# Products with adj in a stack of graph layers: Strassen's four-pass float32 matmuls replaced by three single-pass products of split operands

## The chip, the cores and the metric

The kernel runs on one core of one Trainium2 chip. The metric is the device time of one launch in microseconds (us), lower is better. The profile is one execution taken by the hardware profiler; its span runs from the first to the last instruction.

## What is computed

32 samples of 512 nodes with 128 features go through four layers that share one 512x512 matrix adj. Each layer normalizes x, applies a ReLU, runs a graph network and adds the result to x. Cut to what matters here:

```python
# layer 0: normalized adjacency, then a 128x128 weight
h = relu(layernorm(x));  A = d[:, None] * (adj + eye) * d[None, :]
x = x + einsum('nm,bmc->bnc', A, h) @ W.T + b
# layer 1: five gated steps
h = relu(layernorm(x))
for _ in range(5):
    m = einsum('nm,bmd->bnd', adj, h);  av = concat([m, m])
    z = sigmoid(av @ w3.T + u3(h));  r = sigmoid(av @ w4.T + u3(h))
    hv = tanh(av @ w5.T + (r * h) @ u5.T)
    h = (1 - z) * h + z * hv
x = x + h
# layers 2 and 3: graph attention with masks adj + eye != 0 and adj > 0
```

So a sample needs six products of a 512x512 matrix with a 512x128 one: one with the normalized matrix, five with adj. All inputs and outputs are float32.

## The kernel before, in words

Everything lies in SBUF as tiles of 128 partitions x 512 float32 elements, one tile for one sample. A sample's product with the 512x512 matrix is done for two samples at once, in `products` (line 604). It is Strassen's scheme on 2x2 blocks: VectorE makes four combinations of the two samples' halves (L616), TensorE makes seven block products, each of two matmuls of 128x256 float32 elements (L628), ScalarE copies four partial sums out of PSUM (L633), and VectorE adds three results together (L641). The combinations of the constant matrix are made once by `right_factors` (line 399), for adj and for the normalized matrix. The first four samples of layer 0 use a plain float32 product instead (`product`, L668).

`ggnn` (line 732) runs the five steps of a pair of samples, and `step` (line 755) one step of one sample: gate matmuls (L759, L760), a tanh on ScalarE (L762), r times h on VectorE (L764), matmuls for z (L766) and for the candidate (L773, L774), two more tanh (L768, L776) and three VectorE operations for the new h (L778 to L781). The new h is feature-major and has to be turned for the next product. VectorE turns 32x32 blocks (L570), and DMAs move them through DRAM and back (`shuttle`, line 564). In the first and last steps TensorE turns it instead (`to_features`, L560). `gat` (line 828) does an attention layer; its masked exponentials are L891 and its mixing matmuls L917.

Nothing loops on the chip. The program calls `op(engine, cost, due, emit, reads, writes)` for each piece of work, and `Plan` (line 47) writes out a fixed order for each engine: among the operations whose inputs are there and whose tiles are free, the one with the earliest due slot goes first. Each name in the dictionary at line 274 is a pool of tiles, so its number of tiles limits how far the work of one sample can run ahead. `LANES` (6) limits the samples under way in layer 1. A due of `STEPS * b` puts sample b five slots after the one before it, and each step of a sample six slots (`LANES`) after the last. From `IDLE_FROM` on the planner fills waits of TensorE with transposes of nothing. The order is fixed at build time; on the chip an engine waits on semaphores for the others, and what lies behind a waiting instruction waits too.

The numbers in `op` are the planner's, not measurements. The order in which work for a pair is written is:

```python
for s in range(STEPS):
    now = due + LANES * s
    ms = products(*hs, of_adj, now)
    for i, b in enumerate(pair):
        hs[i], hTs[i] = step(b, s, ms[i], hTs[i], now + i, lanes[i])
```

Of the kernel before, what the change touches and what calls it, by code (L numbers as in the profile page):

```python
# [11 lines left out]
BF16 = mybir.dt.bfloat16  # L12
# [3 lines left out]
P = 128  # L16
# [8 lines left out]
IDLE_FROM = 1420  # L25
RUN_UP = 8
LANES = 6


class Val:  # L30


    def __init__(self, kind, parts=1):
        self.kind, self.uses, self.t = kind, 0, None
        self.writers, self.readers = [[] for _ in range(parts)], [[] for _ in range(parts)]
# [11 lines left out]
class Plan:  # L47
# [42 lines left out]
    SLOT = 10.3  # L90
# [63 lines left out]
    def attempt(self):  # L154
# [80 lines left out]
        while events:  # L235
            now, _, kind, o = heapq.heappop(events)
            if kind == 2:
                pass
            elif kind == 0:
                busy[o.engine] = False  # L240
                settle(o, True)
            else:
                done += o.id is not None
                settle(o, False)
                for v in o.vals:
                    v.uses -= 1
                    if not v.uses and v.kind:
                        free[v.kind].append(v.t)
            for e in ready:
                start(e)  # L250
# [5 lines left out]
def gnn_stack(ctx: ExitStack, tc: tile.TileContext, a: dict, out: bass.AP):  # L256
# [13 lines left out]
    def flat(t):  # L270
# [6 lines left out]
        "x": tiles(13, TOKENS, "x"),  # L277
        "h": tiles(LANES, [P, 2, 2 * D], "h"),
# [4 lines left out]
        "pair": tiles(3, [P, 2, 2 * D], "pair"),  # L283
        "m": tiles(LANES + 1, TOKENS, "m"),
        "S": tiles(2, [P, 4, 2 * D], "S"),
        "half": tiles(6, [P, 2 * P], "half"),
# [9 lines left out]
        "e": tiles(3, [P, C, N], "e"),  # L296
        "v": tiles(2, TOKENS, "v"),
        "mask": tiles(2, [P, N], "mask", dtype=BF16),
# [6 lines left out]
    }, [(167, 0.1), (181, 0.05)], 1300,  # L305
        IDLE_FROM, lambda v: nc.tensor.transpose(v.t[:, 0, :], ident.t, ident.t))
    op = plan.op
    MM, MM1, TURN = 0.858, 0.224, 0.111
# [13 lines left out]
    def load(name, shape, src, due, queue="SP", cost=0.45, delay=4.7):  # L322
        v = fixed(shape, name)
        q = {"SP": nc.sync, "POOL": nc.gpsimd, "AQ": nc.scalar}[queue]
        op(queue if queue != "AQ" else "ACT", cost, due, lambda: q.dma_start(v.t, src), w=[v], delay=delay)
        return v

# [26 lines left out]
    w0 = load("w0", [P, D], a["L0_gnn_W"], -993.9, delay=5.6)  # L354
# [4 lines left out]
    for k in ("w4", "w3", "w5", "u3", "u5"):  # L359
        src = a[f"L1_gnn_{k}_w"]  # L360
        raw[k] = load(k, [P, src.shape[1]], src, -994.5 if k in ("w4", "w3") else -993.3)
# [12 lines left out]
    adjT = fixed([P, C, N], "adjT", C)  # L374
    deg, dinv = fixed(SMALL, "deg", C), fixed(SMALL, "dinv")
# [23 lines left out]
    def right_factors(mT, due, passing=False):  # L399

        made = Val("e", 4) if passing else fixed([P, C, N], "made", 4)

        def quarter(a, n):
            return mT.t[:, 2 * a:2 * a + 2, n * 2 * P:(n + 1) * 2 * P]
        f = {0: (lambda: quarter(0, 0), mT), 3: (lambda: quarter(1, 0), mT), 5: (lambda: quarter(1, 1), mT)}
        f |= {k: (lambda i=i: made.t[:, i].rearrange("p (k n) -> p k n", k=2), made[i]) for i, k in enumerate((2, 1, 4, 6))}
        for k, u, v in ((2, (0, 1), 0), (1, (1, 1), 2), (4, (1, 1), None), (6, (1, 0), 1)):
            op("DVE", 0.62, due, lambda k=k, u=u, v=v: nc.vector.tensor_sub(  # L410
                f[k][0](), quarter(*u), quarter(0, 1) if v is None else f[v][0]()),
               r=[mT, *([f[v][1]] if v else [])], w=[f[k][1]])
        return f
    of_adj = right_factors(adjT, -3.6)
# [14 lines left out]
    def transposed(dues, *group, then=()):  # L429
# [5 lines left out]
        for i, (parts, _) in enumerate(group):  # L435
            def turns(i=i, parts=parts):
                for k, (v, at, sign) in enumerate(parts):
                    nc.tensor.matmul(p.t[:, i, :], v.t[:, at:at + D], sign.t, start=k == 0, stop=k == len(parts) - 1)
# [109 lines left out]
    def chunk(h, c):  # L548

        if h.kind not in ("h", "pair"):  # L550
            return h.t[:, c, :]
        return h.t.rearrange("p a (f l) -> p a l f", l=2)[:, c // 2, c % 2, :]
# [11 lines left out]
    def shuttle(src, squares, dst, halves, due, soon):  # L564
# [3 lines left out]
        if halves:  # L568
            for a in range(2):
                op("DVE", 0.34, soon, lambda a=a: nc.vector.transpose(  # L570
                    sq.t.rearrange("p q (a j l) -> p a q l j", a=2, l=2)[:, a],
                    flat(src.t).rearrange("p (a l q i) -> p a q l i", a=2, l=2, q=Q)[:, a]), r=[src], w=[sq])
        else:
            op("DVE", 0.61, soon, lambda: nc.vector.transpose(
                sq.t.rearrange("p q (c j) -> p q c j", c=C), flat(src.t).rearrange(squares, c=C, q=Q)), r=[src], w=[sq])
# [3 lines left out]
        if halves:  # L579
            for a in range(2):  # L580
                op("SP", 0.4, due, lambda a=a: nc.sync.dma_start(
                    dst.t[:, a, :].rearrange("p (k f) -> p k f", k=Q),
                    far.t.rearrange("q i k (a f) -> a (q i) k f", a=2)[a]), r=[far], w=[dst[a]], delay=5)
        else:
            op("SP", 0.4, due, lambda: nc.sync.dma_start(
                dst.t if dst.kind != "h" else dst.t.rearrange("p a (k f) -> p (a k) f", k=2), far.t.rearrange("q i k f -> (q i) k f")),
               r=[far], w=[dst], delay=5)

    def shuttle_first(h, hT, due, soon):

        sq, far = Val("sq"), Val("far", Q)
        for a in range(2):
            op("DVE", 0.34, soon, lambda a=a: nc.vector.transpose(
                sq.t.rearrange("p k (a l i) -> p a k l i", a=2, l=2)[:, a],
                h.t.rearrange("p a (k j l) -> p a k l j", k=Q, l=2)[:, a]), r=[h[a]], w=[sq])
# [8 lines left out]
    def products(h1, h2, factors, due):  # L604

        x1, x2, S = (h1[0], h1[1]), (h2[0], h2[1]), Val("S", 4)
        HV, HM, HA = 0.34, 2 * 0.432, 0.26

        def part(item):
            v, a = item
            return v.t[:, a, :]

        def combine(o, u, v, f):
            op("DVE", HV, due - 5, lambda: f(part(o), part(u), part(v)), r=[u, v], w=[o])  # L616
        add, sub = nc.vector.tensor_add, nc.vector.tensor_sub
        combine(S[2], x1[0], x2[0], sub)
        combine(S[0], x2[0], x2[1], add)
        combine(S[1], S[0], x1[0], sub)  # L620
        combine(S[3], x1[1], S[1], sub)
        m1, m2, p1, u2, u4, r, t = Val("m", 2), Val("m", 2), Val("half"), Val("half"), Val("half"), Val("bank"), Val("bank")

        def times(r, item, k, fresh, *also):
            def two():
                u = part(item).rearrange("p (f l) -> p l f", l=2)
                for l in range(2):
                    nc.tensor.matmul(low(r), u[:, l, :], factors[k][0]()[:, l, :], start=fresh and l == 0, stop=l == 1,  # L628
                                     skip_group_check=not fresh)
            op("PE", HM, due, two, r=[item, factors[k][1]], w=[r, *also])  # L630

        def copy(o, r, out):
            op("ACT", HA, due - 6, lambda: nc.scalar.copy(out(), low(r)), r=[r], w=[o])  # L633

        def low(v):
            return flat(v.t)[:, :2 * P]

        def high(v):
            return flat(v.t)[:, 2 * P:]
        def add_up(o, u, out):  # L640
            op("DVE", HV, due - 5, lambda: nc.vector.tensor_add(out(), u.t, low(t)), r=[u, t], w=[o])  # L641

        times(r, x1[0], 0, True, m1, m2, t, p1, u2, u4)
        copy(p1, r, lambda: p1.t)
        times(t, x1[1], 3, True)
        add_up(m1[0], p1, lambda: low(m1))
        times(r, S[1], 1, False)
        copy(u2, r, lambda: u2.t)
        times(t, S[2], 4, True)
        times(r, S[0], 2, False)  # L650
        copy(u4, r, lambda: u4.t)
        add_up(m2[1], u4, lambda: high(m2))
        times(t, x2[1], 6, False)
        add_up(m2[0], u2, lambda: low(m2))
        times(r, S[3], 5, False)
        copy(m1[1], r, lambda: high(m1))
        return m1, m2

# [15 lines left out]
    def normalized(begun):  # L674

        anT = fixed([P, C, N], "anT", C)
        drow = Val("bank")
# [15 lines left out]
        return anT, right_factors(anT, -16.5, True)  # L693
# [4 lines left out]
    def gcn(pair, due):  # L698
        first, ys = pair[0] < 4, []
        for i, b in enumerate(pair):  # L700
            y = Val("y", C) if first else Val("pair", 2)
# [8 lines left out]
        ms = [product(y, due + i) for i, y in enumerate(ys)] if first else products(*ys, factors["an"], due + 1)  # L710
        if b == 1:
            factors["anT"], factors["an"] = normalized(ms[0])
# [19 lines left out]
    def ggnn(pair, due):  # L732
        hs, hTs, lanes = [], [], []
        for b in pair:
            lane, h, hT = Val("lane"), Val("h", 2), Val("hT", Q)
# [280 lines left out]
```

The softmax here doesn't subtract the row's maximum and nothing guards it: scores larger than these inputs give would overflow.

## Time and profile before

| | |
|---|---|
| median of 3 runs | 1618.6 us (1618.34 to 1618.92) |
| span of the profiled execution | 1616.2 us |
| TensorE clock granted | 1.000 of full speed |
| VectorE records, start to end | 1379.3 us busy |
| ScalarE records, start to end | 723.0 us busy |
| share of the 16 DMA engines by queue q1 | 39.9% |
| instructions | 24006 |

The profiled execution's span is 2.4 us shorter than the median of the runs; times out of the profile are compared with 1616.2, and the forecast adds the difference. A row of a group reads: line, engine, operation, names written and read, shapes, count, then the busy time in us and the mean in ns of one, then the idle time just before these instructions and what ended it. The ends of matmul records are modelled, so their starts carry more than their lengths. A float32 matmul appears as two records. In the windows a line gives a stretch, its length, the busy time and the count of each of five engines, the clock, the DMA share and GB/s.

### The profile page before, as it was taken

The numbers are of one execution on the slowest core, as the hardware profiler recorded it, in microseconds if no ns is written. First come the engines' busy times: TensorE is split into PE (matmuls) and PEld (weight loads), VectorE is DVE, ScalarE is ACT, GpSimd is POOL, SyncE is SP. The second block draws the span as 40 slices with busy tenths as digits, with TensorE's granted clock in tenths as the row PEclk, the third lists the DMA queues.
The fourth block names the chain that finished last, engine by engine and source line by source line (L and its number), as shares of the span: only waits on it lengthen the run. The fifth ranks groups of instructions, "written<-read, shape, count | busy, mean of one in ns | idle before, by whom it ended". The sixth has DMA issues, their size and how long they took to land.

```text
span 1616.2 us, 24006 instructions
## 1 busy us (share of the span) xinstructions
PE 1609.5 (100%) x7314; PEld 1166.0 (72%) x7314; DVE 1379.3 (85%) x3981; ACT 723.0 (45%) x1622; POOL 143.1 (9%) x137
## 2 busy tenths in 40 slices
PE   9999999999999999999999999999999999999998
PEld 8676667777767777777777767767767767667778
DVE  8977687888898988888989788998887978888888
ACT  5644444535354354443545345353353444443444
POOL 2210000110000001001001011010000100000000
PEclk9999999999999999999999999999999999999999
DMA  4233453443444444363543535445354353434111
GB/s 131 46 85 83 100 129 87 116 108 96 120 97 117 101 122 100 92 143 82 118 110 87 136 86 119 100 98 127 92 118 98 79 124 83 101 98 118 34 33 41
DMA packets 382850, 159.83 MB, mean 99 GB/s; under 512 B 208288, under 2 KB 364288, under 8 KB 382720
## 3 DMA queue, kind: packets, MB, share of 16 engines
q1 hardware_dynamic: 382432, 157.77, 39.9%
q8 instruction: 58, 0.95, 0.3%
q14 instruction: 72, 0.59, 0.1%
q10 hardware_dynamic: 288, 0.52, 0.1%
HBM read 87.30 MB, written 70.89 MB: 98 GB/s over the span
## 4 chain that ended last, share of the span: by engine, by line
PE 96%; DVE 2%; DMA 1%; ACT 0%; issue 0%; SPq 0%; DVEq 0%; ACTq 0%
PE bank L628 35%; PE bank L917 12%; PE bank L759 8%; PE bank L760 8%; PE bank L774 8%; PE bank L766 8%; PE bank L773 8%; PE bank L849 3%; PE bank L718 2%; PE bank L668 1%; PE bank L903 1%; DVE e L891 1%; PE bank L560 1%; DMA e<-in_adj_dram 0%; DMA maskT<-far_mask 0%
## 5 line engine op out<-in xcount | busy, mean ns | idle before, releaser
L493 POOL TENSOR_TENSOR rstd<-ve,mhalf 128x4 f32<-128x4 f32 x119 | 131.8, 1108 | 1375.9 <-DVE ve L485 1054.9
L628 PE MATMUL bank<-made,S 128*128 128x256 f32 x960 | 231.4, 380 | 0.1
L917 PEld LDWEIGHTS bank<-h_gat,e 128*128 128x128 f32 x1792 | 210.2, 191 | 16.4 <-issue 13.6
L917 PE MATMUL bank<-h_gat,e 128*128 128x129 f32 x1792 | 211.9, 275 | 0.0
L633 ACT COPY half<-bank 128x256 f32<-128x256 f32 x282 | 104.2, 370 | 238.7 <-PE bank L628 237.0
L628 PEld LDWEIGHTS bank<-made,S 128*128 128x128 f32 x960 | 184.1, 196 | 31.4 <-issue 12.0
L762 ACT ACTIVATE r<-bank,gate_bw 128x512 f32<-128x512 f32 x160 | 109.5, 685 | 192.5 <-PE bank L760 168.4
L778 DVE TENSOR_TENSOR hv<-hv,hT 128x512 f32<-128x512 f32 x160 | 109.4, 684 | 76.7 <-ACT hv L776 76.5
L776 ACT ACTIVATE hv<-bank,gate_bw 128x512 f32<-128x512 f32 x160 | 109.5, 684 | 127.3 <-PE bank L774 121.6
L759 PE MATMUL bank<-m,wT 128*128 128x512 f32 x320 | 163.6, 593 | 0.0
L766 PE MATMUL bank<-m,wT 128*128 128x512 f32 x320 | 163.4, 592 | 0.0
L774 PE MATMUL bank<-rh,wT 128*128 128x512 f32 x320 | 163.4, 592 | 0.0
L760 PE MATMUL bank<-hT,wT 128*128 128x512 f32 x320 | 163.4, 592 | 0.0
L773 PE MATMUL bank<-m,wT 128*128 128x512 f32 x320 | 163.4, 592 | 0.0
L891 DVE SCALAR_TENSOR_TENSOR e<-row,h_gat,maskT 128x512 f32<-128x512 f32 x224 | 160.1, 738 | 0.0
L764 DVE SCALAR_TENSOR_TENSOR rh<-r,hT 128x512 f32<-128x512 f32 x160 | 109.6, 685 | 58.4 <-ACT r L762 57.0
L628 PE MATMUL bank<-adjT,h 128*128 128x256 f32 x640 | 158.5, 379 | 0.0
L628 PEld LDWEIGHTS bank<-adjT,h 128*128 128x128 f32 x640 | 123.4, 196 | 26.7 <-issue 15.1
L641 DVE TENSOR_TENSOR m<-half,bank 128x256 f32<-128x256 f32 x282 | 115.8, 411 | 30.6 <-ACT half L633 15.7
L768 ACT ACTIVATE z<-bank,gate_bw 128x512 f32<-128x512 f32 x160 | 109.5, 684 | 59.3 <-PE bank L766 56.7
L480 DVE BATCH_NORM_STATS2 st<-x 128x6 f32<-128x128 f32 x480 | 115.6, 277 | 6.8 <-DMA x<-in_x_dram 6.6
L760 PEld LDWEIGHTS bank<-hT,wT 128*128 128x128 f32 x320 | 60.8, 190 | 76.5 <-issue 76.0
(144 smaller groups left out, 2353.4 us busy)
## 6 DMA issues: line engine op xcount, KB each, us to landing
far<-sq SPq DMA_DIRECT2D x936, 64.0 KB
h<-far SPq DMA_DIRECT2D x244, 128.0 KB
gT<-far SPq DMA_DIRECT2D x56, 256.0 KB
row<-line SPq DMA_DIRECT2D x56, 256.0 KB
x<-in_x_dram SPq DMA_DIRECT2D x32, 256.0 KB
hT<-far SPq DMA_DIRECT2D x112, 64.0 KB
h<-far SPq DMA_DIRECT2D x28, 256.0 KB
out_dram<-x SPq DMA_DIRECT2D x28, 256.0 KB
```

What stands on the lines that cost most here:

```text
L480: op("DVE", 0.21, due, lambda c=c: nc.vector.bn_stats(st.t[:, c, :], xb.t[:, c, :]), r=[xb[c]], w=[st[c]])
L493: op("POOL", 1.0, due, lambda: nc.gpsimd.tensor_tensor(rstd.t, ve.t, mhalf.t, ALU.pow), r=[ve, mhalf], w=[rstd])
L628: nc.tensor.matmul(low(r), u[:, l, :], factors[k][0]()[:, l, :], start=fresh and l == 0, stop=l == 1, skip_group_check=not fresh)
L641: op("DVE", HV, due - 5, lambda: nc.vector.tensor_add(out(), u.t, low(t)), r=[u, t], w=[o])
L759: nc.tensor.matmul(flat(gate.t), gates.t[:, 0, :], flat(m.t), start=True, stop=False)
L760: nc.tensor.matmul(flat(gate.t), gates.t[:, 1, :], flat(hT.t), start=False, stop=True)
L764: op("DVE", V, due - 5, lambda: nc.vector.scalar_tensor_tensor(flat(rh.t), flat(r.t), 1.0, flat(hT.t), op0=ALU.add, op1=ALU.mult), r=[r, h ...
L766: op("PE", MM, due + 0.3, lambda: nc.tensor.matmul(flat(gate.t), gates.t[:, 2, :], flat(m.t), start=False, stop=True, skip_group_check=Tru ...
L773: nc.tensor.matmul(flat(cand.t), gates.t[:, 3, :], flat(m.t), start=True, stop=False)
L774: nc.tensor.matmul(flat(cand.t), u5T.t[:, 0, :], flat(rh.t), start=False, stop=True)
L891: op("DVE", 0.68, due + 3, lambda j=j: nc.vector.scalar_tensor_tensor(e.t[:, j, :], rows(row.t), h.t[:, j, D + 1:D + 2], mask(j), op0=ALU. ...
L917: nc.tensor.matmul(pt()[:, c, :D + 1], e.t[:, j, i * P:(i + 1) * P], h.t[:, j, :D + 1], start=(j == 0), stop=(j == C - 1))
```

## The change

Strassen's scheme goes. Each operand of a product is split exactly into an upper part (its first twelve significant bits, by an integer AND with -4096) and a lower part (the rest). Three products are made of these parts, of a type that TensorE multiplies in one pass, float32r: upper x upper, lower x (4096 x lower), and a mixed one, across x across. The sum of the first two is multiplied by 1 + 1/4096 in PSUM by ScalarE, the third is accumulated on top, and the sum is the product. Products are made for one sample, not for two.

Core of the diff:

```diff
-    def right_factors(mT, due, passing=False):
...
+    def factors_of(mT, name, due):
+        upper, lower, across = [fixed([P, C, N], name + k, C, dtype=F32R) for k in ("1", "2", "3")]
+        for c in range(C):
+            cut = Val("cut")
+            op("DVE", 0.35, due, lambda c=c, cut=cut: nc.vector.tensor_scalar(
+                flat(cut.t).bitcast(I32), mT.t[:, c, :].bitcast(I32), UPPER, None, op0=ALU.bitwise_and), r=[mT], w=[cut])
+            op("ACT", A, due, lambda c=c, cut=cut: nc.scalar.copy(upper.t[:, c, :], flat(cut.t)), r=[cut], w=[upper[c]])
+            op("DVE", V, due, lambda c=c, cut=cut: nc.vector.tensor_sub(
+                lower.t[:, c, :], mT.t[:, c, :], flat(cut.t)), r=[mT, cut], w=[lower[c]])
+            op("ACT", A, due, lambda c=c: nc.scalar.mul(
+                lower.t[:, c, :], lower.t[:, c, :].bitcast(F32), SPLIT), w=[lower[c]])
+            op("DVE", V, due, lambda c=c, cut=cut: nc.vector.tensor_sub(
+                across.t[:, c, :], lower.t[:, c, :].bitcast(F32), flat(cut.t)), r=[lower[c], cut], w=[across[c]])
+        return upper, lower, across
...
-    def products(h1, h2, factors, due):
...
+    def in_three(h, turned, factors, due):
+        cut, upper, lower, across = Val("cut"), Val("upper"), Val("lower"), Val("across")
+        upper_of, lower_of, across_of = factors
+        def rows(t, c):
+            return t.rearrange("p k (j c) -> p c (k j)", c=C)[:, c] if turned else t[:, c, :]
+        op("DVE", 0.35, due - 5, lambda: nc.vector.tensor_scalar(
+            flat(cut.t).bitcast(I32), flat(h.t).bitcast(I32), UPPER, None, op0=ALU.bitwise_and), r=[h], w=[cut])
+        op("ACT", A, due - 5, lambda: nc.scalar.copy(flat(upper.t), flat(cut.t)), r=[cut], w=[upper])
+        op("DVE", V, due - 5, lambda: nc.vector.tensor_sub(flat(lower.t), flat(h.t), flat(cut.t)), r=[h, cut], w=[lower])
+        op("DVE", V, due - 5, lambda: nc.vector.scalar_tensor_tensor(
+            flat(across.t), flat(cut.t), 1 + 1 / SPLIT, flat(h.t), op0=ALU.mult, op1=ALU.subtract), r=[h, cut], w=[across])
+        p, m = Val("bank"), Val("m")
+        def times(left, right, first):
+            for c in range(C):
+                nc.tensor.matmul(flat(p.t), rows(left.t, c), right.t[:, c, :], start=first and c == 0, stop=c == C - 1,
+                                 skip_group_check=True)
+        def first_two():
+            times(upper, upper_of, True)
+            times(lower, lower_of, False)
+        op("PE", 8 * MR, due, first_two, r=[upper, lower, upper_of, lower_of], w=[p])
+        op("ACT", A, due - 6, lambda: nc.scalar.mul(flat(p.t), flat(p.t), 1 + 1 / SPLIT), w=[p])
+        op("PE", 4 * MR, due, lambda: times(across, across_of, False), r=[across, across_of], w=[p, m])
+        op("ACT", A, due - 6, lambda: nc.scalar.copy(flat(m.t), flat(p.t)), r=[p], w=[m])
+        return m
```

What goes with it: pools for `cut`, `upper`, `lower` (two tiles each) and `across` (three) in place of `S`, `half` and `pair`; `m` has two tiles in place of seven, `x` nine in place of thirteen, and four more x tiles are handed over when the last reader of `adjT` is done; `e` has two in place of three. `shuttle` makes one transpose of 512 columns and one DMA back in place of two of each. `ggnn` takes one sample, so that the second sample of a pair has a due of its own. The masks are bytes in place of bfloat16, and those of the last samples are made in `masks`, after the third pair's first product, not near the end. The planner's numbers change: `IDLE_FROM` from 1420 to 1342, `SLOT` from 10.3 to 9.7, the start of the end phase from 1300 to 1228.

```diff
-        "x": tiles(13, TOKENS, "x"),
-        "h": tiles(LANES, [P, 2, 2 * D], "h"),
+        "x": tiles(9, TOKENS, "x"),
+        "h": tiles(6, TOKENS, "h"),
...
-        "m": tiles(LANES + 1, TOKENS, "m"),
-        "S": tiles(2, [P, 4, 2 * D], "S"),
-        "half": tiles(6, [P, 2 * P], "half"),
+        "m": tiles(2, TOKENS, "m"),
...
-        ggnn((b, b + 1), STEPS * b)
+        for i in (b, b + 1):
+            ggnn(i, STEPS * i)
```

## The prediction

> **What bounds the kernel now.** I read the page from the top: busy times, then the chain of work that ended last.
>
> ```profile
> PE 1609.5 (100%) x7314; PEld 1166.0 (72%) x7314; DVE 1379.3 (85%) x3981; ACT 723.0 (45%) x1622; POOL 143.1 (9%) x137
> ```
> ```profile
> PE 96%; DVE 2%; DMA 1%; ACT 0%; issue 0%; SPq 0%; DVEq 0%; ACTq 0%
> PE bank L628 35%; PE bank L917 12%; PE bank L759 8%; PE bank L760 8%; PE bank L774 8%; PE bank L766 8%; PE bank L773 8%; PE bank L849 3%; PE bank L718 2%; PE bank L668 1%; PE bank L903 1%; DVE e L891 1%; PE bank L560 1%; DMA e<-in_adj_dram 0%; DMA maskT<-far_mask 0%
> ```
> TensorE is the bound, and Strassen's products (L628) are 35% of the chain. A busy matmul row is not yet a pace, since matmuls overlap; the chain in order of time gives the pace (start, length, records):
>
> ```profile
> 245.03 3.57 PE bank L917 x32
> 251.21 7.78 PE bank L628 x36
> ```
> 7.78 / 36 = 0.216 us for one record of L628, 3.57 / 32 = 0.112 for one of L917. A float32 matmul leaves two records, each with its own weight load. The groups by shape:
>
> ```profile
> L628 PE MATMUL bank<-made,S 128*128 128x256 f32 x960 | 231.4, 380 | 0.1
> L641 DVE TENSOR_TENSOR m<-half,bank 128x256 f32<-128x256 f32 x282 | 115.8, 411 | 30.6 <-ACT half L633 15.7
> ...
> L633 ACT COPY half<-bank 128x256 f32<-128x256 f32 x282 | 104.2, 370 | 238.7 <-PE bank L628 237.0
> ...
> L616 DVE TENSOR_TENSOR S<-S,h 128x256 f32<-128x256 f32 x80 | 33.2, 415 | 0.5
> ...
> L385 ACT COPY adjT<-bank 128x512 f32<-128x512 f32 x4 | 2.2, 582 | 0.6 <-PE bank L383 0.5
> L418 DVE TENSOR_SCALAR mask<-adjT 128x512 bf16<-128x512 f32 x8 | 3.2, 415 | 0.4 <-DMA far_mask<-mask 0.4
> ```
> Next the windows (PE, PEld, DVE, ACT, POOL busy, clock, DMA), for the engine that stands second, VectorE:
>
> ```profile
> 10.00:20.00 10.00, 10.00 (x69) 8.73 (x68) 9.18 (x48) 5.32 (x13) 3.09 (x3) 1.00 0.70 181
> 20.00:30.00 10.00, 10.00 (x65) 8.83 (x64) 9.69 (x40) 7.59 (x18) 3.13 (x3) 1.00 0.30 86
> 30.00:40.00 10.00, 10.00 (x41) 6.92 (x40) 9.93 (x44) 3.07 (x8) 1.72 (x2) 1.00 0.01 2
> ...
> 600.00:800.00 200.00, 200.00 (x892) 144.13 (x891) 175.39 (x506) 88.32 (x194) 18.64 (x17) 1.00 0.44 108
> ```
> PE has no gap in either stretch, but DVE is full between 10 and 80 us and at 88% later. Last, the timeline of DVE, for what an instruction really holds it:
>
> ```profile
> 819.04 0.42 DVE L616 TENSOR_TENSOR S<-pair,pair 128x256 f32<-128x256 f32 x1
> 819.38 0.42 DVE L616 TENSOR_TENSOR S<-pair 128x256 f32<-128x256 f32 x1
> ...
> 821.66 0.74 DVE L891 SCALAR_TENSOR_TENSOR e<-row,h_gat,maskT 128x512 f32<-128x512 f32 x1
> 822.32 0.68 DVE L779 SCALAR_TENSOR_TENSOR hv<-z,hv 128x512 f32<-128x512 f32 x1
> 822.92 0.74 DVE L891 SCALAR_TENSOR_TENSOR e<-row,h_gat,maskT 128x512 f32<-128x512 f32 x1
> ```
> The next one starts about 0.08 before a record ends: 0.34 from start to start for 256 columns, 0.60 for 512. I use these paces for DVE. Each group's count times its pace, over all groups, is 1323 us (82% of the span).
>
> **What the Trainium skill says.** "FP8 and Floating Point Precision", TensorE Precision Notes: true FP32 takes four passes of the array, and reduced FP32 reads four bytes and truncates to FP22. The trace agrees on the four: two records of 0.216 for 256 columns, so 512 column steps each. No run yet shows the one pass. "TensorE: Matmul & The Clock Gate", Part 1: a warm matmul of 512 columns starts 215.7 ns after the one before; the 0.216 above agrees. The same page, LDWEIGHTS: a load takes its columns / 1.2 ns, 107 ns for 128; L917 shows load and matmul together at 0.112, so a load fits behind a matmul of 0.216. "VectorE: DVE Perf Modes", the perf-mode tier table: fp32 tensor_scalar in SBUF runs at 2x, tensor_tensor at 1x. L418 at 415 ns against 684 of L778 agrees.
>
> **The change, part by part.**
>
> *PE.* Before: 94 pairs x 14 matmuls x 2 records x 0.216 = 568.5 us. After: 188 samples x 12 matmuls of 512 columns, one record each. Unknown is one such record: at least 0.216 (its 512 columns), at most 0.43 (two passes, like one record of L759). I take 0.216, since only one pass is asked for and the load (0.112) is covered; a step of 16 bytes in the turned operand adds little (loads with 8-byte steps are 196 ns long, plain ones 190). 2256 x 0.216 = 487.3, so -81.2. Two shuttles become PE transposes (the slot numbers now count single samples): 8 x 0.11 = +0.9.
>
> *DVE.* Removed: 376 combinations x 0.335 + 282 additions x 0.331 = 219. Added per product: a cut, by L418's pace 0.33 (bounds 0.33 and 0.60, if the integer AND gets no 2x; I take 0.33), a subtraction and a multiply-subtract at 0.60: 1.53 x 188 = 288. Factors: eight chunks x 1.53 = 12.3 for eight subtractions of 0.60, +7.5. Transposes: 300 halves x 0.361 become 148 whole ones x 0.63, -15. Sum +61: 1384 us, 89% of the new span. It costs nothing while PE is later; it counts where DVE was full.
>
> *ACT.* Removed: 376 copies x 0.25. Added: 188 x (copy from SBUF 0.60, as L388's 632 ns record, multiply in PSUM at most L385's 0.58, copy out 0.48, the start-to-start pace of L385) and 16 factor passes of 0.6. The sum is +226 on 723: 61% of the span, covered by the same idle time.
>
> *The new wait.* The third product accumulates on a bank that ACT has first multiplied, so it waits about 0.9 us (0.1 + 0.58 + release). In the built program's order I summed PE work between the two groups of each bank: 188 cases, twice 0, twice 0.86, otherwise 1.7 and more, median 7.9. So it is covered outside the head; uncovered it would cost 188 x 0.9 = 169. The gate matmuls' wait for the copy of m has the same 0.9: outside the head 0 twice, 0.86 or 0.89 seven times: +2. On ACT the copy `upper` waits for DVE's cut, with tanh of other samples queued behind; on DVE `lower` waits for one of two buffers, with `rh` behind.
>
> *The head.* DVE and ACT now make three factors a chunk, for adj and the normalized one, with ACT's multiply between two DVE steps, while one sample alone is under way. I walked the order between first use of the adj factors and the second sample's gates, with DVE 6.3 us behind its own running sum (4.8 until x lands, 1.5 of waits). PE waits: first cut and `upper` 2.7; multiply 0.9; copy of m 0.9; tanh behind four factor passes 2.4; `rh` behind six factor steps 0.7; second `upper` 1.4, multiply 0.9, copy 0.4. Sum 10. A check: DVE's running sum up to the `lower` that PE needs at its own sum of 46 is 51.6; with the later start (DVE 6.3, PE 3.3) PE is 8.5 late. Bounds: 5 (the waits overlap work I have put too early) and 20 (the slow AND, more blocking). PE never gets this back, as it is full afterwards.
>
> *Tail.* Near the end the order holds 18 filler transposes in a row, absent before: PE waits there, 18 x 0.11 = +2.
>
> *At nothing.* The eight compares for the last samples' masks move from the end to about 200 us (3.5 us of DVE; that stretch has DVE at 55 of 80 us; uncovered 3.5). Byte masks: L891 stays at one element a cycle. One read-back DMA of 256 KB instead of two of 128 KB: fewer issues on SP. The x pool has 9 tiles until adjT's four are handed over, after those compares; loads are issued up to 20 slots ahead, so this delays loads, not PE; uncovered, one norm waits as long as the first x takes to land (4.8 us). Fewer m buffers (two for seven): each is held for some 6 us of the 47 that a sample takes per six products.
>
> Sum against the profiled execution: 1616.2 - 81.2 + 0.9 + 10 + 2 + 2 = 1549.9. The median lies 2.4 above that span: **1552.3**.
>
> **Rivals.**
> *No loss in the head* (the order has filler where I see none): 1552 - 10 = 1542, at best 1538. For it: PE had no gap there before. Against: the walk. Chance 0.13.
> *DVE and ACT couple to PE all along.* Each product crosses DVE, ACT, PE, ACT, PE, ACT; at 0.25 us lost per product, 47 us: 1599. For it: DVE at 88% in records. Against: no PE gap before under nearly that load, and DVE's running sum leads PE's by 30 us at 250 and by over 100 at 1240. Chance 0.19, from 1567 to 1615.
> *The single-pass matmul is not worth 0.216* (slower). Place: the new line of the products. At two passes it is 2256 x 0.216 = +487: 2040; a weight load left uncovered (0.107) gives +241: 1793. It decides from (1618.6 - 1552) / 2256 = 30 ns more, so 0.246 a matmul. For it: no row shows this type. Against: L759's records at 0.43 are two passes. Chance 0.07. That the change does not do what it says (a type that still takes several passes) is this same case.
>
> **How the numbers follow.** Forecast 1552 with 1543 to 1567: 0.59. Faster by over 0.2% (3 us, what a measurement of this kernel can tell): 0.59 + 0.13 + 0.19 = 0.91; within: 0.02; slower: 0.07. The range for 8 in 10 reaches over the head rival and into the coupled one: 1540 to 1590.
>
> **What would show it.** Right: records of 512 columns at 0.216, about 487 us of the chain for the products, gaps of PE within 25 to 60 us summing to about 10, steady windows without gaps, DVE near 89%. Wrong: a pace over 0.22 in the chain; PE gaps behind `lower` or `upper` after 200 us; a cut record of 680 ns.

## The result and the profile after

The changed kernel takes 1607.4 us (median of 4 runs, 1606.8 to 1608.6) beside 1618.5 for the kernel before: a ratio of 0.9933, with an interval of 0.9919 to 0.9947. It is 11 us faster where 66 were forecast, and lies outside the range of 1540 to 1590. The profiled execution has a span of 1606.8 us; the other three runs have spans of 1604.9 to 1605.8. Below, a pace is the time from the start of one instruction to the start of the next; a step is the distance in memory between neighbouring elements that an instruction reads or writes. A turned h is read with a step of four float32 elements, 16 bytes.

First the page of the kernel after: the busy times and the chain that ended last, by engine and by line.

```profile
PE 1589.5 (99%) x6966; PEld 1160.8 (72%) x6966; DVE 1481.0 (92%) x3751; ACT 905.6 (56%) x1822; POOL 152.5 (9%) x137
PE 90%; DVE 7%; ACT 1%; issue 1%; POOL 0%; DMA 0%; DVEq 0%; ACTq 0%; POOLq 0%
PE bank L623 32%; PE bank L885 11%; PE bank L729 8%; PE bank L730 8%; PE bank L743 8%; PE bank L744 8%; PE bank L736 8%; PE bank L818 3%; PE bank L693 2%; PE bank L871 1%; DVE sq L584 1%; DVE e L859 1%; PE bank L576 0%; DVE hT L751 0%; DVE hv L748 0%
```

TensorE is still the bound. The products (L623 now) are 32% of the chain, some 514 us, where the forecast had 487. DVE has 7% of the chain where it had 2%: it is later than before. The chain in order of time (start, length, records) gives the pace:

```profile
76.96 7.47 PE bank L623 x32
...
350.83 4.74 PE bank L623 x20
```

7.47 / 32 = 0.233 us for a matmul where no operand is turned, and 4.74 / 20 = 0.237 where 16 of the 20 read a turned h. None is at 0.216. From start to start over the whole trace, inside a run of products, the 1440 matmuls with a turned h have a median of 0.236 and a mean of 0.238; the other 816 (the 336 with the normalized matrix and 480 with adj) have 0.233. The groups by shape show what differs:

```profile
L584 DVE STREAM_TRANSPOSE sq<-hT 128x512 f32<-128x512 f32 x148 | 163.6, 1105 | 0.2
...
L623 PEld LDWEIGHTS bank<-adj,across 128*128 128x128 f32 x640 | 156.2, 280 | 41.6 <-issue 22.4 <-ACT bank L630 3.5 <-ACT z L738 1.2
...
L613 DVE TENSOR_SCALAR cut<-h 128x512 int32<-128x512 int32 x160 | 66.5, 416 | 1.3 <-ACT upper L615 0.4 <-ACT h L518 0.3 <-ACT h L762 0.2
...
L584 DVE STREAM_TRANSPOSE sq<-y 128x512 f32<-128x512 f32 x56 | 39.4, 704 | 5.7 <-ACT y L518 5.6
...
L623 PEld LDWEIGHTS bank<-an,lower 128*128 128x128 f32 x112 | 21.1, 188 | 5.2
```

The same transpose of 512 columns takes 1105 ns when it writes every fourth element (`sq<-hT`) and 704 when it writes contiguously (`sq<-y`). The record of a weight load is 188 ns long for a plain operand (`an`) and 280 on average for adj, where one load in four is plain too: those read with a step of 16 bytes are at 309 (median). The cut, at 416, is as forecast. What a long transpose holds DVE, from the timeline:

```profile
612.38 1.10 DVE L584 STREAM_TRANSPOSE sq<-hT 128x512 f32<-128x512 f32 x1
613.32 0.69 DVE L617 SCALAR_TENSOR_TENSOR across<-cut,h 128x512 fp32r<-128x512 f32 x1
```

From start to start 0.94 us (median of 142 also 0.944), where the forecast had 0.63. Last the windows (PE, PEld, DVE, ACT, POOL busy, clock, DMA), for the head and the steady part:

```profile
20.00:30.00 10.00, 9.39 (x64) 8.11 (x63) 9.62 (x38) 6.81 (x16) 2.69 (x2) 1.00 0.11 30
30.00:40.00 10.00, 8.38 (x38) 5.21 (x37) 9.97 (x32) 6.64 (x16) 1.01 (x1) 1.00 0.00 1
40.00:80.00 40.00, 34.90 (x122) 21.39 (x123) 39.07 (x119) 30.13 (x60) 6.33 (x6) 1.00 0.17 33
600.00:800.00 200.00, 200.00 (x862) 146.07 (x860) 188.45 (x479) 114.40 (x229) 21.40 (x18) 1.00 0.43 109
```

PE now has gaps between 20 and 80 us, as forecast, and none in the steady stretch. So most of the missing 55 us do not stand as waits: they are in matmuls that are themselves slower.

A short wait leaves no gap, though. The record of a float32 matmul of 512 columns is 0.59 us long at a pace of 0.43, so a wait of up to 0.16 us hides in it. I therefore also counted from start to start: what PE needs between 100 and 1450 us beyond 0.233 for a product matmul and beyond the paces of the other matmuls. It is 17.7 us in the changed kernel (1.6 in the kernel before, with 0.216). About 11.7 of them stand in products of turned h that have no gap around them: that is the step. The other 6 are late starts, about half of them visible as gaps. The experiments below use this count.

### The profile page after: what moved, and what is told of

The parts are those of the page before. It is cut to its first block, busy times and chain, and to the rows that moved or that the text cites. A ratio compares the mean times of both kernels' runs of the same rounds, so it can differ in the third digit from the quotient of the medians.

```text
span 1606.8 us, 23090 instructions
## 1 busy us (share of the span) xinstructions
PE 1589.5 (99%) x6966; PEld 1160.8 (72%) x6966; DVE 1481.0 (92%) x3751; ACT 905.6 (56%) x1822; POOL 152.5 (9%) x137
## 4 chain that ended last, share of the span: by engine, by line
PE 90%; DVE 7%; ACT 1%; issue 1%; POOL 0%; DMA 0%; DVEq 0%; ACTq 0%; POOLq 0%
PE bank L623 32%; PE bank L885 11%; PE bank L729 8%; PE bank L730 8%; PE bank L743 8%; PE bank L744 8%; PE bank L736 8%; PE bank L818 3%; PE bank L693 2%; PE bank L871 1%; DVE sq L584 1%; DVE e L859 1%; PE bank L576 0%; DVE hT L751 0%; DVE hv L748 0%
## 5 line engine op out<-in xcount | busy, mean ns | idle before, releaser
L623 PE MATMUL bank<-adj,across 128*128 128x512 f32 x640 | 215.3, 462 | 1.6 <-ACT bank L630 1.6
L630 ACT ACTIVATE bank<-bank 128x512 f32<-128x512 f32 x188 | 109.3, 581 | 186.2 <-PE bank L623 183.6
L623 PE MATMUL bank<-adj,upper 128*128 128x512 f32 x640 | 201.2, 436 | 1.3 <-ACT upper L615 1.3
L623 PEld LDWEIGHTS bank<-adj,across 128*128 128x128 f32 x640 | 156.2, 280 | 41.6 <-issue 22.4
L623 PE MATMUL bank<-adj,lower 128*128 128x512 f32 x640 | 177.0, 398 | 0.0
L623 PEld LDWEIGHTS bank<-adj,upper 128*128 128x128 f32 x640 | 154.4, 280 | 30.1 <-issue 8.8
L584 DVE STREAM_TRANSPOSE sq<-hT 128x512 f32<-128x512 f32 x148 | 163.6, 1105 | 0.2
L623 PEld LDWEIGHTS bank<-adj,lower 128*128 128x128 f32 x640 | 152.9, 280 | 7.2
L615 ACT CAST upper<-cut 128x512 fp32r<-128x512 f32 x188 | 115.2, 613 | 45.7 <-DVE cut L613 44.3
L632 ACT COPY m<-bank 128x512 f32<-128x512 f32 x188 | 109.9, 586 | 53.8 <-PE bank L623 53.3
```

What stands on the lines that cost most here:

```text
L584: op("DVE", 0.61, soon, lambda: nc.vector.transpose(sq.t.rearrange(f"p q {inner} -> p q c j", c=C), flat(src.t).rearrange(squares, c=C, q= ...
L615: op("ACT", A, due - 5, lambda: nc.scalar.copy(flat(upper.t), flat(cut.t)), r=[cut], w=[upper])
L623: nc.tensor.matmul(flat(p.t), rows(left.t, c), right.t[:, c, :], start=first and c == 0, stop=c == C - 1, skip_group_check=True)
L632: op("ACT", A, due - 6, lambda: nc.scalar.copy(flat(m.t), flat(p.t)), r=[p], w=[m])
```

## The experiments

In all of them "before" ran beside at 1618.3 to 1618.5. Every ratio is against it.

**1. halves.** Each product matmul issued as two of 256 columns, with the same weights loaded twice.

```diff
-                nc.tensor.matmul(flat(p.t), rows(left.t, c), right.t[:, c, :], ...)
+                for a in range(2):
+                    nc.tensor.matmul(flat(p.t)[:, a * 2 * P:(a + 1) * 2 * P], rows(left.t, c), right.t[:, c, a * 2 * P:(a + 1) * 2 * P], ...)
```

> Every product matmul of 512 columns is issued as two of 256 with the same weights (24 for 12 in a product). Theory 1, the float32r stream is slow by the column (0.233 us for 512): 24 x 0.1165 = 2.80 us a product as now, 1607 within 5 us. Theory 2, each single-pass matmul carries a fixed extra of about 0.018 us (a load or hand-over that one pass no longer hides): 24 x (0.107 + 0.018) = 3.0 us a product, about 1645. A record shorter than 0.12 us speaks for theory 1.

1920.3 us, ratio 1.1864 (1.1844 to 1.1883): far from both times that were expected, since neither theory had a limit in the loads. Its chain in order of time, first products without a turned operand, then products of turned h:

```profile
76.71 7.61 PE bank L624 x64
...
205.87 5.49 PE bank L624 x24
```

7.61 / 64 = 0.119 for half the columns: two such are 0.238 beside the 0.233 of a whole one. So the single-pass pace goes with the columns, some 0.445 ns each and 5 ns a matmul, not with an extra fixed cost (which would give 0.108 + 0.017 = 0.125). It also says that a plain load, which comes with each of these matmuls, needs no more than 0.119 and can't be what sets 0.233. The turned operand does not halve at all: 5.49 / 24 = 0.229 (median of all 0.233). There the weight load sets the pace. A load with a 16-byte step takes about 0.23 us, longer than the 0.216 in which the forecast wanted to hide it.

**2. bf16.** The parts stored as bfloat16 in place of float32r. This leaves out the low bits of each part.

```diff
-F32R = mybir.dt.float32r
+F32R = mybir.dt.bfloat16
```

> The upper, lower and mixed parts are stored as bfloat16 in place of float32r, so low bits are left out; the instructions and their order stay. Theory 1, the pace of 0.233 to 0.236 belongs to the four-byte single-pass type: 0.216 here, 2256 x 0.019 = 43 us less, about 1564. Theory 2, any single pass of 512 columns has it, as the weight load is not hidden: about 1607.

1579.5 us, ratio 0.976 (0.9745 to 0.9774). The chain and a group of loads:

```profile
954.18 2.59 PE bank L623 x12
```
```profile
L623 PEld LDWEIGHTS <-lower 128*128 128x128 bf16 x752 | 81.0, 108 | 81.3
```

2.59 / 12 = 0.216, which is also the median of the whole trace, and loads of 108 ns on average (100 plain, 113 with the step, which is 8 bytes here). The forecast's pace is that of two-byte operands. But 28 us came back, not 43: PE's gaps after 120 us sum to 21 us here (5 in the changed kernel). DVE is at 93%; that it can't keep up with a faster PE is tested in bf16_squares.

**3. plain_rows.** The product reads its stationary operand with step 1, which leaves the features in another order.

```diff
-            return t.rearrange("p k (j c) -> p c (k j)", c=C)[:, c] if turned else t[:, c, :]
+            return t[:, c, :]
```

> The turned operand's weights are read with a step of one element, so the features of a turned sample are taken in another order; nothing else changes. Theory: the 16-byte step of the weight loads (records of 309 ns against 188) costs only the 0.236 - 0.233 that the layer-0 products, which have plain weights, show: about 1200 x 0.003 = 4 us, 1603. Rival: the step is the cause of the slow pace: 0.216, about 1565.

1600.3 us, ratio 0.9888 (0.9873 to 0.9902). Pace 0.233 from start to start, loads 188 ns. 7.0 us came back. The step itself cost more: 1440 x 0.005 = 7 in the pace (means), and 4.3 where a load stands behind a short matmul (below). Most of the rest was given back as late starts of PE: between 100 and 1450 us they grow from some 6 us to 9 (10.5 beyond the paces, about 1 of it in products without a gap).

**4. plain_squares.** The transposes write contiguously, which also leaves the features in another order.

```diff
-            sq.t.rearrange(f"p q {inner} -> p q c j", c=C), flat(src.t).rearrange(squares, c=C, q=Q)), r=[src], w=[sq])
+            sq.t.rearrange("p q (c j) -> p q c j", c=C), flat(src.t).rearrange(squares, c=C, q=Q)), r=[src], w=[sq])
```

> The 32x32 transposes write their blocks next to each other and not with a step of four elements, so a turned sample has its features in another order; the weight loads keep their step. Theory: the transposes fall from about 1.03 to 0.63 us each, 148 x 0.4 = 59 us of VectorE less, and the small gaps of TensorE after 120 us (about 13 us in all) shrink by half or more: 1597 to 1602. Rival: VectorE hides under TensorE anyway: 1607 within 2 us.

1601.7 us, ratio 0.9898 (0.9883 to 0.9913). `sq<-hT` falls from 1105 to 702 ns and DVE's busy time by 40 us, but the end comes 5.6 earlier only: DVE stands beside PE, and its time counts where it is late. Between 100 and 1450 us PE needs 12.2 us beyond the paces, 10.5 of them the step's: of the 6 us of late starts fewer than 2 are left.

**5. bf16_squares.** bfloat16 parts and contiguous transposes together (low bits left out, features in another order).

```diff
-F32R = mybir.dt.float32r
+F32R = mybir.dt.bfloat16
...
-            sq.t.rearrange(f"p q {inner} -> p q c j", c=C), flat(src.t).rearrange(squares, c=C, q=Q)), r=[src], w=[sq])
+            sq.t.rearrange("p q (c j) -> p q c j", c=C), flat(src.t).rearrange(squares, c=C, q=Q)), r=[src], w=[sq])
```

> bfloat16 parts as in the run bf16 (low bits left out), and contiguous transposes as in plain_squares (features of turned samples in another order). Theory: in bf16 TensorE waits for VectorE (gaps of about 21 us after 120 us in place of 5), which is why it won 28 us and not 43. With 59 us less on VectorE most of these gaps go: 1560 to 1567. Rival: the gaps come from the longer chain through ScalarE: 1575 to 1579.

1557.3 us, ratio 0.9623 (0.9607 to 0.9639), span 1553.9. PE's gaps after 120 us fall from 21 us to 9, so DVE was behind most of them. With a pace of 0.216 and transposes at 0.63 the forecast's sum, 1549.9 for the span, is missed by 4 us. That supports the rest of the sum, but doesn't prove each term.

**6. unturned.** The whole computation again, with no step in either place: the transposes write contiguously, the two DVE operations that split h write their result in turned order, and the mixed part is made from these two results. The core of the edit:

```diff
+        def split(t):
+            return t.rearrange("p c (k j) -> p c k j", k=Q) if turned else flat(t)
+        def whole(t):
+            return t.rearrange("p k (c j) -> p c k j", c=C) if turned else flat(t)
...
-            flat(cut.t).bitcast(I32), flat(h.t).bitcast(I32), UPPER, None, op0=ALU.bitwise_and), r=[h], w=[cut])
+            split(cut.t).bitcast(I32), whole(h.t).bitcast(I32), UPPER, None, op0=ALU.bitwise_and), r=[h], w=[cut])
...
-            flat(across.t), flat(cut.t), 1 + 1 / SPLIT, flat(h.t), op0=ALU.mult, op1=ALU.subtract), r=[h, cut], w=[across])
+            flat(across.t), flat(cut.t), 1 / SPLIT, flat(lower.t).bitcast(F32), op0=ALU.mult, op1=ALU.subtract), r=[lower, cut], w=[across])
...
-        shuttle(new, "p (c q i) -> p q c i", h, due, due - 5, "(j c)")
+        shuttle(new, "p (c q i) -> p q c i", h, due, due - 5)
```

> The transposes write contiguous blocks, and the cut and the lower part undo the turn while they split, so that all weights of a product lie contiguous (the mixed part is made from cut and lower part); the whole computation is kept. The two gains found one at a time should add: 7 us for plain weight loads, 6 us for faster transposes, and a little for the final addition to x, which no longer reads with a step of four (28 x 0.4 us of VectorE): 1591 to 1596. Rival: the cut and the subtraction slow down on their four-dimensional patterns and VectorE pays back what it saved: 1600 or more, with cut records well over 420 ns.

1591.0 us, ratio 0.9828 (0.9813 to 0.9842). The groups:

```profile
L628 PEld LDWEIGHTS bank<-adj,lower 128*128 128x128 f32 x640 | 120.2, 188 | 28.8
...
L584 DVE STREAM_TRANSPOSE sq<-hT 128x512 f32<-128x512 f32 x148 | 104.0, 703 | 0.3
L618 DVE TENSOR_SCALAR cut<-h 128x512 int32<-128x512 int32 x160 | 65.5, 412 | 0.9 <-ACT h L767 0.4 <-ACT h L518 0.3
```

Turning in blocks of 32 elements costs the cut nothing (412 ns beside 416), and both steps are gone, with the one in the last addition to x: 16.4 us. Between 100 and 1450 us PE needs 2.3 us beyond the paces in place of 17.7.

**7. late_factors.** The factors of the normalized matrix later, to take four passes from ahead of the first tanh.

```diff
-        return factors_of(anT, "an", -16.5)
+        return factors_of(anT, "an", -2)
```

> The three factors of the normalized matrix get a due of -2 in place of -16.5, so that r times h of the first sample, and the products of the next two, are placed ahead of most of them; the rest of the order is the planner's. Theory: the head's loss (TensorE 71.0 busy of the first 80 us against 78.5 before) comes from factor work ahead of the only samples under way: half of it returns, 1602 to 1604. Rival: it is the chain through cut, multiply and copy, whatever stands beside it: 1606 to 1608.

1608.1 us, ratio 0.9936 (0.9921 to 0.9951): not what was expected. The waits named there did fall (for r from 1.78 to 0.34), but PE then stood once for 4.45 us. Its timeline, and the windows behind it:

```profile
38.17 1.12 PE L736 MATMUL bank<-m,wT 128*128 128x512 f32 x2 [0.34 <-ACT r L732]
...
45.46 1.09 PE L576 MATMUL bank<-ident,hT 128*128 128x128 f32 x4 [4.45 <-DVE hT L751]
```
```profile
46.00:48.00 2.00, 2.00 (x7) 1.44 (x6) 1.93 (x8) 1.24 (x3) 1.40 (x1) 0.50 0.00 0
48.00:50.00 2.00, 2.00 (x7) 1.52 (x6) 2.00 (x10) 1.11 (x3) 0.00 (x0) 0.50 0.03 8
50.00:52.00 2.00, 2.00 (x9) 1.65 (x8) 1.31 (x10) 1.36 (x3) 0.28 (x1) 0.82 0.00 0
```

The loss of the head is one sample's chain, and moving work in it moved the wait. The one long wait was worse than the several short ones: the clock is at 0.50 after it, which costs 2 x 1.0 + 0.36 = 2.4 us more. In the changed kernel no wait is over 1.8 us and the clock stays at 1.00. The Trainium skill, "TensorE: Matmul & The Clock Gate", Part 1, says that the clock falls to half after an idle window of about 3.4 us; this trace agrees.

**8. true_costs.** Only the planner's numbers: 0.236 for a product matmul, 1.03 for a stepped transpose (a record less 0.08; the start-to-start pace of 0.944 would have been the better number).

```diff
-    MM, MM1, TURN, MR = 0.858, 0.224, 0.111, 0.216
+    MM, MM1, TURN, MR = 0.858, 0.224, 0.111, 0.236
...
-        op("DVE", 0.61, soon, lambda: nc.vector.transpose(
+        op("DVE", 0.61 if inner == "(c j)" else 1.03, soon, lambda: nc.vector.transpose(
```

> Only the planner's costs change: 0.236 for a single-pass matmul (0.216) and 1.03 for a transpose with a step (0.61), as measured; the instructions stay, their order changes. Theory: the 5 us of gaps after 120 us come from VectorE being late against an order laid out for shorter work: 2 to 5 us less, 1602 to 1605. Rival: the order is not the cause: 1607 within 2 us.

1602.7 us, ratio 0.99 (0.9886 to 0.9915). The written order assumed a PE and a DVE that the chip doesn't have; telling both numbers is worth 4.7 us. Between 100 and 1450 us 12.2 us are left beyond the paces, 10.1 of them the step's, so most of the late starts are gone.

**9. unturned_costs.** Unturned, with `MR` at 0.234.

> The unturned version (plain weights, plain transposes; 1591.0 us) with the planner told 0.234 us in place of 0.216 for a product matmul, as the records show. Theory 'part of the loss is an order planned for a faster PE': telling true costs took 4.7 us off the changed kernel, so here about 1586 to 1589 (the transposes need no correction here). Rival 'the order is as good as it gets, the rest is pace': 1591 within 1 us.

1585.2 us, ratio 0.9795 (0.9781 to 0.981). 5.8 us off, and the fastest of the versions that leave nothing out.

**10. no_multiply.** Leaves out ScalarE's multiplication in PSUM, so the first two products are not scaled.

```diff
-        op("ACT", A, due - 6, lambda: nc.scalar.mul(flat(p.t), flat(p.t), 1 + 1 / SPLIT), w=[p])
```

> Leaves out ScalarE's multiplication by 1 + 1/4096 in PSUM between the two groups of each product (the first two products are then not scaled); the factors' own multiplications stay. Theory 'the new wait is covered outside the head': 188 x 0.9 us of wait are hidden, so only the head's two waits (about 1 to 2 us) and a little order change go: 1603 to 1607. Rival 'ScalarE's step between the groups couples the engines': at 0.1 to 0.25 us lost per product 19 to 47 us come back: 1588 or less.

1606.6 us, ratio 0.9928 (0.9913 to 0.9942). 0.7 us off with 188 multiplications gone. The order of the head differs too, and has one wait of 5.0 us with the half clock behind it, so in the head the multiplications may be worth a few us more. Outside it nothing came back: 18.5 us beyond the paces between 100 and 1450 us, beside 17.7. The rival's 19 to 47 us are not there.

**11. m_three and 12. mask_one.** Three tiles for m, paid for by one mask tile fewer, and as a control the one mask tile alone.

```diff
-        "m": tiles(2, TOKENS, "m"),
+        "m": tiles(3, TOKENS, "m"),
...
-        "mask": tiles(2, [P, N], "mask", dtype=U8),
+        "mask": tiles(1, [P, N], "mask", dtype=U8),
```

> Three tiles for the products' results m in place of two (paid for by one mask tile fewer). Theory 'two m tiles cost nothing': 1606 to 1609. Rival 'two tiles hold the next product back, in the head above all': 3 to 8 us faster.

> The control for three m tiles: one mask tile in place of two, and still two m tiles. Theory 'two m tiles hold products back': nothing gained, 1606 to 1610. Rival 'any other order of the work is that much better (or the mask tile is what counts)': 1598 to 1603.

m_three: 1599.4 us, ratio 0.9884 (0.9868 to 0.9901). mask_one: 1605.0, ratio 0.9917 (0.9902 to 0.9932). Of the 8.0 us, 2.4 come without the third tile, by the mask tile or the other order that it brings, and 5.6 with it or with the order that the planner then writes. PE's waits between 100 and 1450 us in the changed kernel (line, what it waited for, us, times, longest; two of 0.3 and 0.2 us are left out):

```profile
PE bank L729 <- ACT m L632: 1.5, 2, 0.7
PE bank L743 <- DVE h_gat L836: 0.6, 1, 0.6
PE bank L729 <- DVE h_gat L836: 0.4, 1, 0.4
```

In m_three this list is empty. These waits are 3 us of the gain; the rest lies in late starts that leave no gap. Counted from start to start, m_three needs 11.2 us beyond the paces in this stretch, 10.9 of them the step's, so hardly a late start is left; mask_one still needs 16.1, with 11.2 of the step.

**13. unturned_m_three and 14. costs_m_three.** The third m tile (and one mask tile) in unturned_costs and in true_costs.

> The unturned version with true costs (1585.2 us) and three m tiles (one mask tile). Theory 'two m tiles hold products back, whatever the operands': 3 to 8 us off, 1577 to 1582. Rival 'the gain was the order's, and true costs have it already': 1584 to 1587.

> The changed kernel with true costs for the planner (1602.7 us alone) and three m tiles (1599.4 alone). If the two gains are separate: 1607.4 - 4.7 - 8.0 = 1594 to 1596. If they remove the same waits: 1598 to 1600.

costs_m_three: 1595.4 us, ratio 0.986 (0.9845 to 0.9874): 7.3 us off true_costs, so the two gains add up (12.0 of 12.7). unturned_m_three: 1585.6, ratio 0.9798 (0.9782 to 0.9815): nothing. The expectation that two m tiles hold products back whatever the operands has failed: the third tile helps where DVE is at 92% and 1441 us of pace, and not where it is at 90% and 1385. That points to m as slack against a late DVE, not as a limit of its own: faster transposes (plain_squares), true costs and the third tile each remove most of the same 6 us of late starts. It was not tested apart.

## Why the prediction was wrong

**The step that failed** is "I take 0.216, since only one pass is asked for and the load (0.112) is covered; a step of 16 bytes in the turned operand adds little". One pass is right: 512 columns are one record, and the products fell. But both numbers in it were taken from other operands. The pace is 0.233 for float32r with plain weights (bf16: 0.216) and 0.238 on average with a 16-byte step, where the load takes about 0.23 and sets the pace when the matmul is shorter. So, with the means, 1440 x 0.2378 + 816 x 0.233 = 532.5 in place of 487.3: +45.2. Of the gain of 81 some 36 were left by pace alone. The price of this step was in the bounds (0.216 to 0.43), and the rival on it was to decide at 0.246; at a mean of 532.5 / 2256 = 0.236 two thirds of the way to it were gone. The range counted the two-pass end and left out the small miss: 9% of a term of 487 us is more than the head, the waits and the tail together.

**The same step, exposed.** Behind a short matmul even the whole load doesn't fit. Where a product follows matmuls of 0.11 us, PE takes 0.47 from the last of them to the second product matmul, in place of 0.349: 35 places x 0.12 = +4.3. The timeline of PE in the changed kernel shows one:

```profile
566.35 1.06 PE L818 MATMUL bank<-w_aug,gT 128*128 128x131 f32 x8
567.16 1.30 PE L623 MATMUL bank<-adj,across 128*128 128x512 f32 x4
568.30 0.59 PE L736 MATMUL bank<-m,wT 128*128 128x512 f32 x1
```

Four product matmuls hold PE for 1.14 us here, beside 4 x 0.236 = 0.94. Of the difference 0.08 is the first record, which starts 0.03 after the last short one and not 0.11; the other 0.12 is the load. In plain_rows the same way takes 0.345, so it is the step.

**DVE.** The forecast's 1384 us are 1441: transposes 148 x (0.944 - 0.63) = +46 and the additions of a stepped h to x (1091 ns beside 677) 28 x 0.41 = +11. Cut (0.334) and the 0.60 of the other two were right, and in unturned the sum is 1387. The page "SBUF — State Buffer" of the Trainium skill, "Door 1: The DMA port swizzle", says that SBUF has lines of 16 bytes, that at least two hits on a line are needed for full bandwidth, and that each access to a new line pays a penalty. The traces agree with that, on loads as on DVE: a load's record has 188 ns without a step, 196 with 8 bytes (kernel before), 309 with 16. The forecast looked at the first two and called the third little.

**ACT and the new wait.** ACT is at 56%, where 61% were forecast. The new wait was right: the waits for L630 sum to 1.6 us, in two places, both in the head; no_multiply agrees. The copy of m: 2.5 us in 4 places, beside 1.3 in the head and 2 later as forecast.

**The head.** Right in kind and size. The timeline of PE in the changed kernel:

```profile
35.58 1.20 PE L623 MATMUL bank<-adj,across 128*128 128x512 f32 x4 [0.67 <-ACT bank L630]
37.51 1.12 PE L729 MATMUL bank<-m,wT 128*128 128x512 f32 x2 [0.73 <-ACT m L632]
...
41.71 1.12 PE L736 MATMUL bank<-m,wT 128*128 128x512 f32 x2 [1.78 <-ACT r L732]
...
44.42 1.12 PE L744 MATMUL bank<-rh,wT 128*128 128x512 f32 x2 [0.73 <-DVE rh L734]
46.67 1.20 PE L623 MATMUL bank<-adj,upper 128*128 128x512 f32 x4 [1.12 <-ACT upper L615]
...
49.72 1.20 PE L623 MATMUL bank<-adj,across 128*128 128x512 f32 x4 [0.92 <-ACT bank L630]
...
51.65 1.12 PE L729 MATMUL bank<-m,wT 128*128 128x512 f32 x2 [0.29 <-ACT m L632]
```

0.67, 0.73, 1.78, 0.73, 1.12, 0.92, 0.29 for the forecast's 0.9, 0.9, 2.4, 0.7, 1.4, 0.9, 0.4, in the same order. The 2.7 for the first cut did not show at that place. In all PE is busy for 71.0 of the first 80 us, beside 78.5 before: 7.5 us lost, within the bounds of 5 to 20. Counted from start to start, PE loses 9.8 us between 26 and 80 us (0.3 before). That this is so close to the 10 is partly luck, since the 2.7 is missing and smaller waits fill its place.

**Tail.** The forecast had 18 fillers, 2 us. There are 20 (none before), 2.4 us; PE's gaps after 1400 us grow by 1.8 besides.

**At nothing.** "Fewer m buffers" was wrong in this kernel: up to 5.6 us. The byte masks are right: the masked exponential keeps its pace of 0.662 us. The moved compares, the single read-back DMA and the x pool were not tried apart; no wait of PE after 100 us names one of them.

**The rivals.** "No loss in the head" fell with the list above. "The single-pass matmul is not worth 0.216" was right in its place and short of its deciding point. The measured time lies in the range of "DVE and ACT couple to PE all along", but not for its reason: what DVE and ACT cost PE in the stream is the 6 us of late starts, not 47. So that the time fell in that range is luck for the rival. A stronger coupling of that kind does appear in bf16, where PE is faster.

**The sum anew**, for the span, counted from start to start. The forecast was 1549.9. Pace and exposed loads add 45.2 + 4.3 = 49.5. Small waits outside the head, as gaps or as late starts, grew by 10.3 us where the forecast had 2 (the copy of m): +8.3. The head lost 9.6 more than before, forecast 10: -0.4. The fillers are +0.4, and after PE's last start there are 1.1 us less. That makes 1606.6; the measured span is 1606.8, in an execution about 1 us above the median. So the pace is the first miss and the small waits are the second; most of those in the steady part go when the transposes write without a step (plain_squares). Why a float32r column takes 0.445 ns where a bfloat16 one takes 0.42 stays open: no run separates the moving operand's type from the stationary one's.

## What to carry to other kernels

A pace is that of an operand: of its type and its step in memory, not only of its columns. Before a load is called hidden, find a row that has that step, and if there is none, give the step a bound of its own; on a term that is 30% of the time, 20 ns on each of 2256 matmuls were 45 of the 66 us that were forecast. And when a price turns out otherwise, tell the planner: the order written for the wrong price cost some 5 us here.

## What the runs showed of the hardware

- A float32r matmul of 512 columns is one record, at 0.233 us from start to start; 256 columns are 0.119. In bfloat16 512 columns are 0.216.
- "TensorE: Matmul & The Clock Gate" of the Trainium skill, "LDWEIGHTS", gives a load as its columns / 1.2, 107 ns for 128, and names no type and no step. Loads of bf16 agree, with records of 108 ns. Four-byte loads have records of 188 ns, but these overlap: plain float32 ones follow each other at 0.112 in the attention products (3.57 / 32), plain float32r ones at 0.119 or less (halves). With a step of 16 bytes the records are 309 ns, and the loads follow each other at 0.229 to 0.233 (halves). There the measurement decides.
- A DVE transpose of 128x512 that writes every fourth element takes 0.944 us from start to start, a contiguous one 0.628. A tensor_tensor that reads one operand with that step has a record of 1091 ns in place of 677. Patterns with contiguous blocks of 32 elements cost nothing (412 ns for a cut).
- An integer AND on 128x512 elements with a constant has a pace of 0.334 us, where operations on two tensors of that size have 0.60.
- Behind one wait of PE of 4.45 us the clock was at 0.50 for the next 4 us (late_factors); waits of up to 1.8 us left it at 1.00.
